# One-hot products in fp32 and columns turned through DRAM in the graph stage of a graph-and-experts kernel

## The chip, the cores and the metric

The kernel runs on one core of one Trainium2 chip. The metric is the time of the whole program on the device, in microseconds (us). TensorE is called PE in the profile, VectorE DVE, ScalarE ACT, GpSimd POOL and SyncE SP. The profile is that of one execution; the time before is the median of three runs.

## The reference

The program has two halves. The first adds to x the product of a sparse matrix (67,584 weighted edges between 2048 nodes, sorted by `dst`) with the normalized rows of x, and a bias per node. The second normalizes the result and adds a mixture of eight experts, of which each row uses its two best.

```python
x = x + gnn(layernorm(x), edge_weight, stack([src, dst]), node_vec1)
x = x + experts(layernorm(x), Wr, br, ln_g, ln_b, W1, b1, W2, b2)

def gnn(x, values, indices, bias):          # x [2048, 256]
    row, col = indices[0], indices[1]       # row is src, col is dst
    gathered = values[:, None] * x[col]
    return segment_sum(gathered, row, num_segments=2048) + bias
```

All is fp32. The change is in the first half alone.

## The kernel before

**The idea of the graph stage.** The sparse matrix is built as a dense one, block by block, and multiplied. For each destination node (a column of the matrix) at most KW = 64 edges are looked at. A source number is split into a high part (32 values, HI) and a low part (64 values, LO). For one destination, `hr` is a 64 x 32 table (edge by high part, holding the edge's weight where the high part agrees) and `hl` a 64 x 64 table (edge by low part, holding one). Their product over the edges is the column's 2048 entries as a 32 x 64 table. To be exact in bf16, the weight is cut into three bf16 parts, and three products are added up for each destination: 2048 x 3 = 6144 products. Each uses a quarter of TensorE's columns and half of its rows (`tile_position`), so that eight tiles stand side by side.

**Finding the edges.** The destinations are handled in GQ = 8 groups of 256 (q). For each group a run of 656 entries of `dst` is gathered for each partition (`get_run`), at a place that `find_run` finds from a coarse list of every 528th entry (`first_i`). ScalarE counts with three Sign passes how many entries lie before the destination (`count_before`), `get_win` works out where its edges begin and gathers 64 sources and 64 weights for each of two destinations by indirect DMAs on GpSimd. `keys_of` makes the high part, the low part and the mask, and `turn_keys` transposes them on TensorE, so that edges lie on partitions. `next_part` makes the second and third bf16 part of the weight.

**The loop.** A half-block n (0 to 31) has 64 destinations. `make_hots(n)` makes `hl`, `eq` and `hr` on VectorE (L335, L338, L342). `make_cols(n)` runs 192 products into `pa` (L360) and copies them to `ar` on ScalarE (L364). After two half-blocks, `turn_cols` transposes `ar` within blocks of 32 x 32 on VectorE (L372) to `ac`, a block of 128 destinations by 2048 sources. `dense(g, b)` multiplies the blocks of a group (GROUPS: one or two blocks) by the normalized rows `xn_sb` for the 128 nodes of block b (L379). In the loop at least 8 such products are put after each half-block. `add_later` copies four results to `sum` on ScalarE (L391), and GpSimd adds them to `acc` by an accumulating DMA (L393). The last group is added on VectorE (L385), after the loop, in steps that alternate with the router of the second half. During n = 0 to 3 the rows of x are also transposed, weighed for the router (`weigh_x`) and normalized (`scale_x`).

**Order.** All this stands in a section whose order on every engine is written by hand (`manual_schedule`): each engine runs its instructions in the order of the program text. The constants ahead of it are placed by the framework. The check at n = NH - 3 uses `rows_d`, a copy of `dst` with one entry more per row: it counts where `dst` falls; if the edges were unsorted or a destination had more than 64, a slow path would be taken.

**After the graph stage.** The router, the lists of rows for each expert, and the expert slots follow (L690 on); the first product there is `px` (L839), then `ph` (L1012) and `py` (L1026).

Of the kernel before, what the change touches and what calls it, by code (L numbers as in the profile page):

```python
# [21 lines left out]
P = 128  # L22
# [4 lines left out]
def kernel(  # L27
# [46 lines left out]
    RUN = EJ + P  # L74
    GROUPS = (1, 1, 2, 2, 2, 2, 2, 2, 2)
# [19 lines left out]
    first_i = xpool.tile([P, 1], I32, name="first_i")  # L95
    nc.sync.dma_start(first_i, dst.rearrange("(p j) -> p j", p=P)[:, 0:1])
# [5 lines left out]
    nc.scalar.dma_start(wr_sb, Wr.rearrange("(k p) e -> p k e", p=P))  # L102
    nv_rows = small.tile([NB, P], F32, name="nv_rows", bufs=1)
    nc.scalar.dma_start(nv_rows, node_vec1.rearrange("(b p) o -> b (p o)", p=P))
    for q in range(4):
        s = slice(q * NB // 4, (q + 1) * NB // 4)
        (nc.sync, nc.scalar)[q % 2].dma_start(acc[:, s, :D], xv[:, s, :])
    b1_rows = small.tile([NE * KH, P], F32, name="b1_rows", bufs=1)
    nc.sync.dma_start(b1_rows, b1.rearrange("e (c p) -> (e c) p", p=P))
    g_rows = small.tile([NE * KD, P], F32, name="g_rows", bufs=1)  # L110
    nc.sync.dma_start(g_rows, ln_g.rearrange("e (k p) -> (e k) p", p=P))
    be_rows = small.tile([NE * KD, P], F32, name="be_rows", bufs=1)
    nc.sync.dma_start(be_rows, ln_b.rearrange("e (k p) -> (e k) p", p=P))
    br_sb = consts.tile([P, NE], F32, name="br_sb")
    nc.scalar.dma_start(br_sb, bass.AP(tensor=br.tensor, offset=br.offset, ap=[[0, P], [1, NE]]))
    rows_d = xpool.tile([P, EJ + 1], I32, name="rows_d")
    nc.vector.memset(rows_d[:, EJ:], N)
    flat = lambda n: bass.AP(tensor=dst.tensor, offset=dst.offset, ap=[[EJ, P - 1], [1, n]])
    nc.sync.dma_start(rows_d[:P - 1, :], flat(EJ + 1))
    nc.sync.dma_start(rows_d[P - 1:, :EJ], dst.rearrange("(p j) -> p j", p=P)[P - 1:, :])  # L120


    ident = consts.tile([P, P], F32, name="ident")
# [9 lines left out]
    iota_p = consts.tile([P, P], F32, name="iota_p")  # L133
    nc.gpsimd.iota(iota_p, pattern=[[1, P]], base=0, channel_multiplier=0,
                   allow_small_or_imprecise_dtypes=True)
    eps_sb = consts.tile([P, 1], F32, name="eps_sb")
    nc.vector.memset(eps_sb, EPS)
# [19 lines left out]
    cols_d = dram.tile([NE, P, KH + 2 * KD], F32, name="cols_d")  # L157
    none = consts.tile([P, RW], F32, name="none")
# [13 lines left out]
    firsts = consts.tile([P, P], F32, name="firsts")  # L172
    nc.gpsimd.iota(firsts, pattern=[[P, 2], [GH // 2, 2], [GH, 4], [GC, GM]], base=0,
                   channel_multiplier=0, allow_small_or_imprecise_dtypes=True)
    col_q = consts.tile([P, GQ], F32, name="col_q")
    nc.gpsimd.iota(col_q, pattern=[[GC * P, GQ]], base=0, channel_multiplier=0,
                   allow_small_or_imprecise_dtypes=True)
    own_p = consts.tile([P, P], F32, name="own_p")
    col_p = consts.tile([P, 1], F32, name="col_p")
    nc.vector.scalar_tensor_tensor(own_p, firsts, 1.0, ident, op0=OP.mult, op1=OP.mult,  # L180
                                   accum_out=col_p)
    col0 = consts.tile([P, GQ], F32, name="col0")
    nc.vector.tensor_scalar(col0, col_q, col_p, None, op0=OP.add)
    edge = consts.tile([P, GQ, 3], F32, name="edge")
    nc.vector.tensor_tensor(edge, col0[:, :, None].to_broadcast([P, GQ, 3]),
                            iota_p[:, None, :3].to_broadcast([P, GQ, 3]), OP.add)
    nc.vector.tensor_scalar(edge, edge, -0.5, None, op0=OP.add)

    cols_1 = gnn.enter_context(tc.tile_pool(name="cols_1", bufs=GROUPS[-1]))
    ps_s = gnn.enter_context(tc.tile_pool(name="ps_s", bufs=3, space=PSUM))
    edges = gnn.enter_context(ExitStack())
    cols_0 = edges.enter_context(tc.tile_pool(name="cols_0", bufs=6))
    pool = lambda name, bufs, **k: edges.enter_context(tc.tile_pool(name=name, bufs=bufs, **k))
    find = pool("find", 1)
    one_d = lambda t: t.rearrange("(e o) -> e o", o=1)
    wins = [None] * GQ
    runs = [None] * GQ
    used_q = find.tile([P, GQ, GC], F32, name="used_q")  # L200
    less = find.tile([P, GQ], F32, name="less")
    base = find.tile([P, GQ], F32, name="base")
    base_i = find.tile([P, GQ], I32, name="base_i")
    mid = find.tile([P, GQ], F32, name="mid")
# [8 lines left out]
    def find_run(pf, q):  # L213
        junk = find.tile([P, P], F32, name="less_1")
        nc.vector.tensor_scalar(junk, pf, col0[:, q:q + 1], None, op0=OP.is_lt, op1=OP.add,
                                accum_out=less[:, q:q + 1])

    def get_runs(q0, q1, q2):
        r = slice(q0, q1)
        nc.vector.tensor_scalar(base[:, r], less[:, r], -1.0, 0.0, op0=OP.add, op1=OP.max)  # L220
        nc.vector.tensor_scalar(base[:, r], base[:, r], float(EJ), float(E - RUN), op0=OP.mult,
# [3 lines left out]
        for q in range(q0, q2):  # L225
            get_run(q)
# [10 lines left out]
    def count_before(q, ends=range(3)):  # L237
        for i in ends:
            sign = find.tile([P, RUN], BF16, name="sign")
            nc.scalar.activation(sign, runs[q], AF.Sign, bias=edge[:, q, i:i + 1], scale=-1.0,  # L240
                                 accum_out=signs[:, q, i:i + 1])

    def get_win(q):
        nc.vector.scalar_tensor_tensor(at[:, q, :], signs[:, q, :], 0.5,
# [103 lines left out]
    def make_cols(n, hl, hr):  # L348
# [3 lines left out]
        if h == 0:  # L352
            ars[cb] = rowsp.tile([P, HI, LO], F32, name="ar")
# [837 lines left out]
```

## Time and profile before

| | us |
|---|---|
| median of three runs | 598.04 (594.74 to 598.71) |
| the profiled execution, its own time | 603.62 |
| its span, first to last instruction | 601.8 |
| first one-hot product (L360) | 34.0 |
| last dense products of the graph stage end | 312.9 |

| engine | busy us | share |
|---|---|---|
| PE | 492.3 | 82% |
| PE weight loads | 416.7 | 69% |
| DVE | 306.1 | 51% |
| ACT | 241.8 | 40% |
| POOL | 176.3 | 29% |

How to read it: busy times are summed over the span, and matmuls are pipelined, so a busy PE is not a PE at its peak. A group of the profile names its line, engine and operation, what is written and read, and then busy time, mean time of one in ns, and the idle time just before its instructions with what ended that ("<-issue" is time in which the engine waited for nothing that the profile shows). PEclk is the granted share of TensorE's clock.

### The profile page before, as it was taken

Reading aid. Unit: us, or ns where it says so; the run is one execution under the profiler, and the core shown is the slowest. Engines: PE = TensorE matmul, PEld = TensorE weight load, DVE = VectorE, ACT = ScalarE, POOL = GpSimd, SP = SyncE. Lnnn points to the kernel's source line nnn. Section 1 sums busy time; section 2 is a strip of 40 time slices with the busy share of each in tenths; the row PEclk is TensorE's granted clock in tenths of the full one; section 3 lists DMA queues with packets and bytes.
Section 4 is the critical chain, followed back from the end, with each engine's and each line's share of the span. In section 5 each row is a group of like instructions: output and inputs, shape, how many; then the busy total and the mean of one; then the engine's idle time right before and its main releaser. Section 6 shows DMA issues by size and latency. Waiting matters only on the chain. (4 is left out here: it accounts for less than half of the span.)

```text
span 601.8 us, 18439 instructions
## 1 busy us (share of the span) xinstructions
PE 492.3 (82%) x8070; PEld 416.7 (69%) x8070; DVE 306.1 (51%) x678; ACT 241.8 (40%) x547; POOL 176.3 (29%) x165
## 2 busy tenths in 40 slices
PE   1168787487887697689989999999999989994792
PEld 1157665476676575567868788888888878883682
DVE  5675977878786776674586642222232232220101
ACT  2436575346364443233593733333333333331220
POOL 2253034234242311111103343333344423431121
PEclk9998588599899897989979999999999999997797
DMA  6011277244444432532995269766689967748332
GB/s 196 20 56 35 43 144 148 40 103 82 100 78 82 84 76 52 98 66 59 248 386 173 43 206 339 227 184 188 200 255 361 312 146 209 186 129 240 104 88 98
DMA packets 55486, 88.53 MB, mean 147 GB/s; under 512 B 8274, under 2 KB 43330, under 8 KB 55330
## 3 DMA queue, kind: packets, MB, share of 16 engines
q1 hardware_dynamic: 40946, 55.20, 27.8%
q0 software_dynamic: 12944, 30.95, 25.6%
q8 instruction: 67, 1.10, 0.8%
q10 hardware_dynamic: 1504, 1.07, 0.6%
q14 instruction: 25, 0.20, 0.1%
HBM read 60.65 MB, written 11.36 MB: 120 GB/s over the span
## 5 line engine op out<-in xcount | busy, mean ns | idle before, releaser
L379 PE MATMUL py<-xn_sb,ac 128*128 128x264 f32 x512 | 144.4, 440 | 8.6 <-ACT sum L391 6.2
L379 PEld LDWEIGHTS py<-xn_sb,ac 128*128 128x128 f32 x512 | 107.7, 217 | 34.3 <-ACT sum L391 10.2
L1012 PE MATMUL ph<-xeT,w 128*128 128x256 f32 (+1 forms) x576 | 123.0, 372 | 3.8 <-issue 2.5
L1026 PE MATMUL py<-w,hT 128*128 128x256 f32 x544 | 124.4, 387 | 0.0
L1014 ACT ACTIVATE hT<-ph,ec 128x256 f32<-128x256 f32 (+1 forms) x144 | 66.6, 462 | 133.8 <-PE ph L1012 75.9
L1012 PEld LDWEIGHTS ph<-xeT,w 128*128 128x128 f32 x576 | 106.0, 194 | 18.0 <-issue 5.0
L1026 PEld LDWEIGHTS py<-w,hT 128*128 128x128 f32 x544 | 104.7, 195 | 14.3
L360 PE MATMUL pa<-hl,hr 64*32 64x64 bf16 x6144 | 62.6, 203 | 46.8 <-issue 39.7
L360 PEld LDWEIGHTS <-hr 64*32 64x32 bf16 x6144 | 54.2, 91 | 59.9 <-issue 51.3
L1034 POOL DMA_INDIRECT y_d<-ys,to_i x32 | 51.8, 1620 | 139.3 <-DVE ys L1029 89.5
L393 POOL DMA_DIRECT2D acc<-sum x32 | 28.8, 912 | 156.8 <-ACT sum L391 156.8
L391 ACT COPY sum<-py 128x264 f32<-128x264 f32 x128 | 47.6, 381 | 56.9 <-PE py L379 55.6
L986 DVE TENSOR_SCALAR xeT<-px,ec 128x256 f32<-128x256 f32 (+1 forms) x40 | 19.1, 519 | 94.9 <-PE px L977 92.2
L372 DVE STREAM_TRANSPOSE ac<-ar 128x2048 f32<-128x2048 f32 x16 | 59.5, 3718 | 2.5 <-ACT ar L364 2.5
L1029 DVE SCALAR_TENSOR_TENSOR ys<-py,wt,b2w 128x256 f32<-128x256 f32 x34 | 16.4, 484 | 80.0 <-PE py L1026 73.4
L342 DVE TENSOR_TENSOR hr<-eq,w 128x3072 bf16<-128x3072 bf16 x32 | 56.3, 1758 | 1.1
L944 POOL DMA_INDIRECT xs<-xr_d,to_i x39 | 40.8, 1045 | 52.9 <-DVE z L723 31.2
L364 ACT COPY ar<-pa 128x1024 f32<-128x1024 f32 x32 | 32.3, 1009 | 54.5 <-PE pa L360 54.5
L335 DVE TENSOR_TENSOR hl<-k,iota_b 128x2048 bf16<-128x2048 bf16 x32 | 38.8, 1213 | 27.8 <-PE pa L360 27.5
L1001 ACT ACTIVATE b2w<-b,wt 128x256 f32<-128x256 f32 x37 | 16.8, 500 | 44.4 <-DVE wt L999 39.9
L252 POOL DMA_INDIRECT win_s<-in_src,at_i x16 | 18.6, 1162 | 45.3 <-DVE n_d L262 42.3
L240 ACT ACTIVATE sign<-run,edge 128x656 bf16<-128x656 int32 x24 | 20.4, 848 | 7.7 <-DMA run<-in_dst,base_i 7.2
(205 smaller groups left out, 348.4 us busy)
## 6 DMA issues: line engine op xcount, KB each, us to landing
w<-in_L_ffn_W SPq DMA_DIRECT2D x42, 1024.0 KB, 7.3
acc<-sum POOLq DMA_DIRECT2D x32, 528.0 KB, 5.5
b<-in_L_ffn_b SPq DMA_DIRECT2D x21, 128.0 KB, 8.1
out<-y_d SPq DMA_DIRECT2D x4, 512.0 KB, 5.3
xr_d<-rec SPq DMA_DIRECT2D x1, 1300.0 KB, 7.6
y_d<-acc SPq DMA_DIRECT2D x1, 1280.0 KB
acc<-in_x SPq DMA_DIRECT2D x2, 512.0 KB, 6.1
acc<-in_x ACTq DMA_DIRECT2D x2, 512.0 KB, 7.9
```

Source lines behind the costliest of these rows:

```text
L335: nc.vector.tensor_tensor(hl.rearrange("p g (n t) -> p g n t", t=2), two(k2[:, 0], g, LO), pair(iota_b, LO), OP.is_equal)
L342: nc.vector.tensor_tensor(hr.rearrange("p g i (n t) -> p (g i) n t", t=2), eq[:, :, None, :].to_broadcast([P, GH, 3, HI]), w[:, :, None, : ...
L360: nc.tensor.matmul(pa[c * HI:(c + 1) * HI, j, m * LO:(m + 1) * LO], hr[k, c * GM + m, i, :], hl[k, c * GM + m, :], start=(i == 0), stop=(i ...
L364: nc.scalar.copy(ars[cb][:, h * HI // 2:(h + 1) * HI // 2, :].rearrange("p (m j) l -> p j m l", j=GC), pa.rearrange("p j (m l) -> p j m l" ...
L372: nc.vector.transpose(acs[cb].rearrange("p h l -> p l h"), ars[cb].rearrange("p d l -> p l d"))
L379: nc.tensor.matmul(pa[:, :DX], acs[c].rearrange("p h l -> p (h l)")[:, b * P:(b + 1) * P], xn_sb[:, c, :], start=(c == group_of[g][0]), st ...
L391: nc.scalar.copy(sums_of[0][:, k, :], pa[:, :DX])
L944: nc.gpsimd.indirect_dma_start(out=(sets[s.set][0] if into is None else into)[:, t, :], out_offset=None, in_=(xr_d if rows is None else ro ...
L1012: nc.tensor.matmul(ph, w1[:, k, c * P:(c + 1) * P], xeT[:, k, :], start=(k == 0), stop=(k == KD - 1))
L1014: nc.scalar.activation(hT[:, c, :s.n * P], ph, AF.Gelu, bias=ec[:, c:c + 1], scale=1.0)
L1026: nc.tensor.matmul(py, hT[:, c, t * P:(t + 1) * P], w2[:, c, :], start=(c == 0), stop=(c == KH - 1))
L1034: st = nc.gpsimd.indirect_dma_start(out=y_d[:, :], out_offset=bass.IndirectOffsetOnAxis(ap=tos[s.to][:, t:t + 1], axis=0), in_=ys, in_offs ...
```

## The change

- One product in fp32 for each destination replaces the three in bf16. `hl` is made in bf16 (`hb`) and widened to fp32 by ScalarE; `hr` is fp32. `next_part` and the bf16 parts go.
- A half-block is made in two halves (`make_cols(n, 0)` and `make_cols(n, 1)`), with dense products after each of them (QUOTA = 8 in all). The dense results are added by VectorE (`add`), not by ScalarE and an accumulating DMA. GROUPS has larger last groups, and a group becomes ready LAG = 4 half-blocks after its last block began.
- The columns are turned through DRAM (`move_cols`): SP stores `ar` to `ad`, and reads it back in four parts of 16 rows, in pieces of 64 elements.
- Destinations are in plain order (`col0`, `base` from iota). Runs of q = 0 are read at fixed places (`run_0`, STEP apart) by SP, and `count_before`, `locate` and `get_half` work on one edge at a time; the other runs are shorter (264 + 128 entries) and found from a list of every 264th entry.
- Loads of the start are in another order on SP and ACT; the memset of the last column of `rows_d` stands after its load. Statistics and scaling of x are done four blocks at a time inside the loop, and `node_vec1` is added by GpSimd.

```diff
-    RUN = EJ + P
-    GROUPS = (1, 1, 2, 2, 2, 2, 2, 2, 2)
+    EH = EJ // 2
+    RUN = EH + P
+    STEP = E // NG
+    BACK = 4 * STEP
+    RUN_0 = 2 * BACK + P
+    LAG = 4
+    QUOTA = 8
+    GROUPS = (1, 1, 2, 2, 3, 3, 4)
...
+    nc.sync.dma_start(run_0[nf:, :], part(dst, 0, STEP, P - nf, RUN_0))
+    nc.sync.dma_start(run_0[:nf, :], part(dst, 0, 0, nf, RUN_0))
+    nc.sync.dma_start(first_i, bass.AP(tensor=dst.tensor, offset=dst.offset, ap=[[EJ, P], [EH, 2]]))
...
+    get_x(nc.sync, 0)
+    get_x(nc.scalar, 1)
+    nc.sync.dma_start(wr_sb, Wr.rearrange("(k p) e -> p k e", p=P))
     nc.sync.dma_start(b1_rows, b1.rearrange("e (c p) -> (e c) p", p=P))
     nc.sync.dma_start(g_rows, ln_g.rearrange("e (k p) -> (e k) p", p=P))
     nc.sync.dma_start(be_rows, ln_b.rearrange("e (k p) -> (e k) p", p=P))
+    nc.sync.dma_start(nv_rows, node_vec1.rearrange("(b p) o -> b (p o)", p=P))
+    get_x(nc.sync, 2)
+    get_x(nc.sync, 3)
+    nc.sync.dma_start(br_sb, bass.AP(tensor=br.tensor, offset=br.offset, ap=[[0, P], [1, NE]]))
-    nc.vector.memset(rows_d[:, EJ:], N)
-    nc.sync.dma_start(rows_d[:P - 1, :], flat(EJ + 1))
+    nc.sync.dma_start(rows_d[:P - 1, :], part(dst, 0, EJ, P - 1, EJ + 1))
     nc.sync.dma_start(rows_d[P - 1:, :EJ], dst.rearrange("(p j) -> p j", p=P)[P - 1:, :])
...
+    nc.vector.memset(rows_d[:, EJ:], N)
...
     def make_hots(n):
-        hl = hotl.tile([P, GH, LO], BF16, name="hl")
-        nc.vector.tensor_tensor(hl.rearrange("p g (n t) -> p g n t", t=2),
+        hb = hotl.tile([P, GH, LO], BF16, name="hb")
+        nc.vector.tensor_tensor(hb.rearrange("p g (n t) -> p g n t", t=2),
                                 two(k2[:, 0], g, LO), pair(iota_b, LO), OP.is_equal)
+        hl = hotl.tile([P, GH, LO], F32, name="hl")
+        casts.append(lambda: nc.scalar.copy(hl, hb))
         eq = hotr.tile([P, GH, HI], BF16, name="eq")
...
-        hr = hotr.tile([P, GH, 3, HI], BF16, name="hr")
...
+        hr = hotr.tile([P, GH, HI], F32, name="hr")
+        nc.vector.tensor_tensor(hr, eq, w_t[:, g * GH:(g + 1) * GH, None]
+                                .to_broadcast([P, GH, HI]), OP.mult)
...
-    def make_cols(n, hl, hr):
+    def make_cols(n, i, hl, hr):
+        if i == 0:
+            halves_of[n] = (ps_a.tile([P, GC, GM * LO], F32, name="pa"),
+                            rowsp.tile([P, GM, GC, LO], F32, name="ar"))
+        pa, ar = halves_of[n]
+        ms = range(i * GM // 2, (i + 1) * GM // 2)
+        for m in ms:
+            for c in range(4):
+                for j in range(GC):
+                    k = slice(j * KW, (j + 1) * KW)
+                    nc.tensor.matmul(pa[c * HI:(c + 1) * HI, j, m * LO:(m + 1) * LO],
+                                     hr[k, c * GM + m, :], hl[k, c * GM + m, :],
+                                     start=True, stop=True, tile_position=(j * KW, c * HI))
+        ms = slice(ms.start, ms.stop)
+        nc.scalar.copy(ar[:, ms].rearrange("p m j l -> p j m l"),
+                       pa.rearrange("p j (m l) -> p j m l", l=LO)[:, :, ms])
+
+    def move_cols(n):
+        cb, h = n // 2, n % 2
+        ar = halves_of.pop(n)[1]
+        ad = dram.tile([P, GM * GC, LO], F32, name="ad", bufs=4)
+        nc.sync.dma_start(ad, ar.rearrange("p m j l -> p (m j) l"))
+        if h == 0:
+            acs[cb] = (cols_1 if cb >= NB - GROUPS[-1] else cols_0).tile([P, HI, LO], F32, name="ac")
+        for c in range(4):
+            d = h * P // 2 + c * GM * GC
+            nc.sync.dma_start(acs[cb][d:d + GM * GC],
+                              ad[c * HI:(c + 1) * HI].rearrange("h k l -> k h l"))
...
-    def turn_cols(cb):
-        nc.vector.transpose(acs[cb].rearrange("p h l -> p l h"),
-                            ars[cb].rearrange("p d l -> p l d"))
...
-    def add_later(b, pa):
...
+    for q in range(2, GQ):
+        find_run(pf, q)
+    place_runs()
+    get_run(1)
+    get_run(2)
+    cols, wc = turn_columns()
+    block_stats(bn, mv, acc, range(0, 2))
+    turn_x(0)
+    turn_x(2)
+    turn_keys(0, keys_of(0))
...
+        for n in range(NH + 1):
+            while late:
+                add(*late.pop(0))
+            if n < NH:
+                make_cols(n, 0, *hots[n])
+            if n + 1 < NH:
+                hots[n + 1] = make_hots(n + 1)
+                casts.pop()()
+            while ready < last_g and 2 * group_of[ready][-1] + LAG <= n:
+                jobs += [(ready, b) for b in range(NB)]
+                ready += 1
+            more_dense(n)
+            if n < NH:
+                make_cols(n, 1, *hots.pop(n))
+                move_cols(n)
+            while late:
+                add(*late.pop(0))
+            for s in range(1, GQ):
+                if n == max(4 * s - 6, 0):
+                    count_before(s)
+                if n == max(4 * s - 5, 0):
+                    get_win(s)
+                    if s + 2 < GQ:
+                        get_run(s + 2)
+                if n == 4 * s - 2:
+                    turn_keys(s, keys_of(s))
+            if n < 4:
+                if n:
+                    turn_x(4 * n)
+                    turn_x(4 * n + 2)
+                    block_stats(bn, mv, acc, range(4 * n, 4 * n + 4))
+                scale_x(4 * n, 4)
+                weigh_x(4 * n)
+                weighed_x(4 * n, 4)
+            more_dense(n)
```

In the changed file `run_0` is loaded at L115 and L116, `rows_d` at L145 and L146, its memset is L194, the key transposes are L331 and L332, the one-hot products L370, the ar copy L374, the store L383, the reads L388 and the dense products L395.

## Prediction

> **What bounds the kernel now.** I read the stages first, the busy time of each engine in four stretches:
>
> ```profile
> core 0: us, PE busy (x) PEld busy (x) DVE busy (x) ACT busy (x) POOL busy (x), PEclk, DMA share, GB/s
> 34.00:76.40 42.40, 34.90 (x889) 30.48 (x893) 29.97 (x54) 23.53 (x53) 10.43 (x10) 0.76 0.22 52
> 76.40:285.00 208.60, 164.97 (x5795) 133.03 (x5794) 155.08 (x164) 94.29 (x215) 54.74 (x52) 0.89 0.43 86
> 285.00:313.00 28.00, 24.90 (x109) 20.13 (x110) 18.49 (x44) 19.54 (x50) 2.65 (x5) 0.91 1.02 304
> 313.00:602.00 289.00, 261.92 (x1270) 229.00 (x1269) 81.36 (x316) 93.15 (x204) 96.72 (x75) 0.95 0.66 196
> ```
>
> The change touches the first 313 us: a start of 34 us, half-blocks n = 0 to 3 in 42.4 us, n = 4 to 31 in 208.6 us (7.45 us each), and a tail of 28 us to the first px product. Nothing after that is edited. In the long stretch TensorE and VectorE are both three quarters busy and neither is full, so I read the groups (busy, mean ns of one, idle before it and who ended that) and then TensorE's timeline (start, length, instruction, idle before it):
>
> ```profile
> L379 PE MATMUL py<-xn_sb,ac 128*128 128x264 f32 x512 | 144.4, 440 | 8.6 <-ACT sum L391 6.2
> L360 PE MATMUL pa<-hl,hr 64*32 64x64 bf16 x6144 | 62.6, 203 | 46.8 <-issue 39.7
> L391 ACT COPY sum<-py 128x264 f32<-128x264 f32 x128 | 47.6, 381 | 56.9 <-PE py L379 55.6
> L372 DVE STREAM_TRANSPOSE ac<-ar 128x2048 f32<-128x2048 f32 x16 | 59.5, 3718 | 2.5 <-ACT ar L364 2.5
> L342 DVE TENSOR_TENSOR hr<-eq,w 128x3072 bf16<-128x3072 bf16 x32 | 56.3, 1758 | 1.1
> L364 ACT COPY ar<-pa 128x1024 f32<-128x1024 f32 x32 | 32.3, 1009 | 54.5 <-PE pa L360 54.5
> L335 DVE TENSOR_TENSOR hl<-k,iota_b 128x2048 bf16<-128x2048 bf16 x32 | 38.8, 1213 | 27.8 <-PE pa L360 27.5
> ```
>
> ```profile
> 108.09 1.28 PE L360 MATMUL pa<-hl,hr 64*32 64x64 bf16 x128 [3.94 <-issue]
> 111.82 1.30 PE L360 MATMUL pa<-hl,hr 64*32 64x64 bf16 x128 [2.45 <-issue]
> ...
> 173.59 1.75 PE L360 MATMUL pa<-hl,hr 64*32 64x64 bf16 x192
> ```
>
> Undisturbed, 192 one-hot products take 1.75 us, 8.1 ns from start to start. But 39.7 us are lost to "issue", in bursts of exactly 128 products that begin 3.73 us apart. VectorE in turn waits 27.5 us for these products before hl. So the stretch is bound by the two in turn: VectorE's hl, eq, hr and transposes cost 5.5 us per n, and TensorE's products, when their instructions come late, hold up the next hots.
>
> **What the skill says.** (1) "Runtime: NRT & Kernel Launch", section Instruction fetch mechanics: TensorE's instructions arrive in blocks of 256. The bursts agree: 128 products and 128 weight loads are 256 instructions, and one block takes 3.73 us here. The page calls this mostly hidden; 39.7 us say otherwise. (2) "FP8 and Floating Point Precision", section TensorE Precision Notes: true fp32 is four passes. The trace agrees: an fp32 product is two matmul records (L379 has 512 for 256 products), and 32 records of 256 columns follow each other in 6.91 us, 216 ns each or 0.844 ns a column. (3) "TensorE: Matmul & The Clock Gate", Part 3: products in different tiles overlap, but start in program order. The 8.1 ns agrees, far under the 27 ns that 64 bf16 columns need. (4) "DMA: Bandwidth & Descriptors", section on why a DMA increments its semaphore by 16: a transfer over 127 partitions runs on one DMA engine. The trace agrees (last part of the start, below).
>
> **Products (removed 6144 bf16, added 2048 fp32).** Each fp32 product is two records on the same tile, one after the other. The second can't start until the first has streamed 64 columns at 0.844 ns = 54 ns; the next product is on another tile and may follow a few ns later. So about 54 + 5 = 59 ns per product, whatever the tiles overlap, 64 x 59 = 3.78 us per n. Bounds: 16 ns if the four instructions are limited by issue alone (half of 8.1 ns each); about 86 ns if the second weight load (27 ns) doesn't hide. I take 59: in the full-array stream the next weight load starts beside the running product. Fetch falls from 384 to 256 instructions per n, with the dense products 288, or 4.2 us at 3.73 us per 256: the issue stall goes.
>
> **Steady n (28 of them).** TensorE: 3.78 us of one-hot, 8 dense products of 2 x 221 ns = 3.54 us, and now two changes of tile mode each way instead of one. In the trace the first record after dense to one-hot comes 316 ns on instead of 221, one-hot to dense 127 ns; a round trip is 0.22, two are 0.44. Sum 7.76. By GROUPS, LAG and QUOTA, n = 8, 9, 18, 19 have no dense work; there 6 us. A new stall: at n = 6, 10, ... 26 the key transposes stand between the second half and its dense products, and their f waits for ACT: copy of ar 0.59, two away 0.6, h_1 0.3, then f 0.48 on VectorE, with hand-overs 2.2; the transposes and their mode change 0.8 more; 6 x 3.0 = 18 us. Sum 24 x 7.76 + 4 x 6 + 18 = 228, against 208.6: +19.6.
>
> **Other engines beside it.** VectorE per n: hb 1.21, eq 0.68, hr in fp32 about 1.2 (1024 elements at twice the bf16 slope; bounds 0.7 and 1.8), adds at 0.43 each, 3.4 us at worst (groups of one) and 1.7 with two; keys 0.55: 5.3 to 7.1, under 7.76. The adds are a new wait: they wait for the dense products, and behind them on VectorE stand the hots of n + 1; but these dense products end just before the first half of n, so the hots have all of n. So the 59.5 us of transposes and the smaller hr are freed where they no longer decide. ACT: cast 2048 elements at the slope of its copies (585 ns for 512, 1009 for 1024) 1.86, two ar copies 1.17, keys and signs 1.0: 4.0. The sums on ACT and their accumulating DMAs on POOL (28.8 us) go; POOL's 16 adds of node_vec1 have no row of their kind; between 0.4 us (VectorE's 0.36) and 1.1 (its own iota of that size) each they are hidden, since acc is not added to before n = 4. SP: per n one store of ar (0.4 to issue; stores of 256 to 780 KB landed in 3.9 to 4.1), a wait, four reads of 0.5 each: 0.45 + 4.0 + 2.0 + 0.2 = 6.7 us in a chain, under 7.76 but not by much. The next store stands behind these reads on SP, and ar has two buffers: ACT's ar copy of n + 2 waits for the store of n, and behind that copy stand the cast of hl and the second half's products. So this chain becomes the bound if TensorE is faster than I think. Bandwidth: 2048 pieces of 256 B at 17 ns (window gathers: 138 ns per packet of eight) over 16 engines 2.2 us, and 128 pieces of 4 KB at 159 ns 1.3: half of the time.
>
> **Start.** Reading run 0 at fixed places makes its windows land near 16 us instead of 22. But the memset of rows_d moved behind the load of rows_d, and in VectorE's order it stands among find_run's scans, ahead of place_runs, keys and hots. That load covers 127 partitions:
>
> ```profile
> GB/s 0 2 84 285 328 353 370 362 358 349 128 259 25 23 25 25 23 54 52 30 54 54 6 0 0 0 0 0 0 0 0 33 0 33 0 47 2 33 0 252
> ```
>
> ```profile
> 5.19 0.28 SPq L119 DMA_DIRECT2D rows_d<-in_dst  x1
> 8.71 4.40 SPq L120 DMA_DIRECT2D rows_d<-in_dst  x1
> ```
>
> Slices of 1 us: from 12 us on 25 GB/s is left, one engine's rate; its 127 packets run from 8.8 to 22.0 us. Before, nobody waited. After, it is issued thirteenth on SP, each load from the eighth on waiting for an earlier one: about 8.5, so it lands near 25. Then four scans 2.3, place_runs 0.8, statistics 1.2, keys to k2 3.1 and hots 3.1: first product at 35.5 (was 34.0). n = 0 to 3 are then carried by ACT: 4 x (xn 2.4, xT 1.2, ar 1.2, cast 1.9, small copies 0.5) = 29, signs and keys 6, hand-overs from statistics to sd to rs 1.5 each: 41. So n = 4 starts at 76.5, as before (76.4): no gain.
>
> **Tail.** The last group has 4 columns (64 products) instead of 2 (32). From the last one-hot product: ar copy and store and reads 8.7 us, beside which the rest of n = 31 and three products run; 37 more products for the first ten blocks 16.4; from there to px 10.9, as in the trace (301.7 to 312.7). 36 against 27.7: +8.2.
>
> **Sum.** Start and n = 0 to 3 +0.1, steady +19.6, tail +8.2: +28 on the profiled execution, 603.6 to 632. That execution is 5.6 over the median of the runs shown, so 598 + 28 = 626.
>
> **Rivals.** B, faster: the two records of a product interleave with other tiles', TensorE needs 5 us per n, and SP's chain of 6.7 is the bound: 28 x 6.7 = 188 instead of 228, 586 (557 with stores landing a microsecond sooner). For it: 8.1 ns shows wide overlap, fetch eases. Against: two records of one tile. It decides from about 43 ns per product down, where the 28 us are used up. C, slower still: a product takes 86 ns, 64 x 27 ns x 28 = 48 more, 674; or the reads of 256 B stretch SP's chain to 10 us: 280 + tail, about 678. The dense stream speaks against the first, the gathers' 17 ns against the second. D: rows_d lands before VectorE comes to it; the start gains 11: 615. Against: 13 us on one engine.
>
> **Chances.** Forecast 0.50 (own range 608 to 645), B 0.22, C 0.15, D 0.13. The range leaves out half of B and most of C: 582 to 660. A measurement tells about 1% from no change: faster 0.20 (most of B), within 1% 0.10 (the rest of B, edges), slower 0.70.
>
> **What would show it.** VectorE idle before L194 until about 25 us, the first L370 near 35; L370 starting 59 ns apart on average, no issue gaps; n about 7.8 us; idle of TensorE before L331. I am wrong if 64 products take under 2.8 us, if SP's wait between L383 and L388 exceeds 5 us, or if L194 doesn't wait.

## The result, and the profile after

The changed kernel takes 625.74 us (median of 4 runs, 623.86 to 626.97) beside 596.79 us for the kernel before (4 runs): a ratio of 1.048, 95% interval 1.043 to 1.053. The forecast was 626. The number was right, the main reason for it was not: two errors of the sum cancelled. Ratios and their intervals leave out executions more than 1.5% above the fastest of the same kernel; the medians hold them all.

The profiled execution took 626.97 us with a span of 625.2. The stages come first, cut at the first one-hot product, at n = 4 and at the last one-hot product:

```profile
core 0: us, PE busy (x) PEld busy (x) DVE busy (x) ACT busy (x) POOL busy (x), PEclk, DMA share, GB/s
36.50:75.40 38.90, 30.09 (x603) 26.90 (x603) 22.20 (x65) 28.67 (x57) 22.67 (x21) 1.00 0.55 107
75.40:289.00 213.60, 163.65 (x3957) 121.99 (x3961) 126.88 (x245) 99.98 (x152) 34.63 (x29) 0.86 0.88 141
289.00:325.00 36.00, 19.31 (x115) 15.34 (x105) 5.12 (x14) 4.79 (x15) 0.53 (x3) 0.81 0.98 243
325.00:625.20 300.20, 273.91 (x1344) 239.39 (x1342) 91.14 (x346) 104.28 (x229) 96.50 (x75) 0.96 0.64 191
```

The reader is to see three things. The start up to n = 4 is as long as before (75.4 against 76.4 us). The stretch of n = 4 to 31 takes 213.6 us, only 5 more than before, though TensorE, VectorE and ACT are all less than fully busy; what has doubled is the share of the DMA engines, 0.43 before and 0.88 now (the sum of the packets' times over the time of 16 engines; it can pass 1). And the first px product comes at 339.2 us, 50 us after the last one-hot product, against 28 before. The tail lost 22 us.

The whole profiled executions differ by 23.4 us (601.8 and 625.2), the medians by 29.0: the profiled execution of the kernel before took 603.62 us, 6.8 over its median. So the losses by stage may each be read some microseconds too small.

The waits of the long stretch (engine, line, what it waited for: us in total, times, longest) name the new bound:

```profile
ACT ar L374 <- DMA ad<-ar: 76.1, 17, 6.7
DVE acc L401 <- PE py L395: 64.9, 39, 5.8
PEld pa L370 <- ACT ar L374: 41.7, 21, 4.6
PE pa L370 <- ACT ar L374: 34.6, 16, 4.3
DVE f L321 <- ACT h L317: 11.7, 5, 4.0
```

ACT's copy of ar waits for a store of ar, and TensorE's one-hot products wait for that copy. Why the store is late is on SP's queue (start, length, line, DMAs in a row):

```profile
161.94 2.18 SPq L388 DMA_DIRECT2D ac<-ad  x4
164.22 0.43 SPq L383 DMA_DIRECT2D ad<-ar  x1
169.56 1.89 SPq L388 DMA_DIRECT2D ac<-ad  x4
171.55 0.44 SPq L383 DMA_DIRECT2D ad<-ar  x1
177.46 1.89 SPq L388 DMA_DIRECT2D ac<-ad  x4
179.44 0.43 SPq L383 DMA_DIRECT2D ad<-ar  x1
```

SP never rests for want of work: each store begins 0.1 us after the four reads ahead of it, for every n from 9 on. Between the store and its reads it stands still for 4.5 to 7.2 us, median 5.2, until the store has landed. One round is 0.43 + 5.2 + 1.9 and the small gaps; the stores are 7.96 us apart on average (median 7.90). TensorE's timeline of the same stretch shows what it could do:

```profile
160.26 0.86 PE L370 MATMUL pa<-hl,hr 64*32 64x64 f32 x64
161.05 2.05 PE L395 MATMUL py<-xn_sb,ac 128*128 128x264 f32 x8
163.03 0.86 PE L370 MATMUL pa<-hl,hr 64*32 64x64 f32 x64
...
170.22 0.86 PE L370 MATMUL pa<-hl,hr 64*32 64x64 f32 x64 [1.34 <-ACT ar L374]
...
178.18 0.86 PE L370 MATMUL pa<-hl,hr 64*32 64x64 f32 x64 [2.35 <-ACT ar L374]
```

Where nothing waits, a half of a half-block (32 one-hot products, which are 64 records, and four dense ones) goes from 160.26 to 163.03, 2.77 us, so 5.54 us per n. The 64 records start within 0.643 us, on average 10 ns apart and 20 ns a product. The groups that the sum used (busy, mean ns of one, idle before it) are

```profile
L349 ACT CAST hl<-hb 128x2048 f32<-128x2048 bf16 x32 | 60.8, 1901 | 3.9 <-DVE hb L346 3.8
L370 PE MATMUL pa<-hl,hr 64*32 64x64 f32 x4096 | 63.9, 253 | 43.5 <-ACT ar L374 38.8 <-DVE hr L354 3.7 <-issue 0.7
L354 DVE TENSOR_TENSOR hr<-eq,w_t 128x1024 f32<-128x1024 bf16 x32 | 39.2, 1225 | 4.6 <-PE pa L370 2.6
L374 ACT COPY ar<-pa 128x512 f32<-128x512 f32 x64 | 37.4, 585 | 107.1 <-DMA ad<-ar 76.1 <-PE pa L370 22.3 <-PE py L395 8.6
```

The bursts that end in "issue" are gone, as forecast: 0.7 us of idle time before L370 ends so, against 39.7 before. What stands before L370 now is ACT's copy, and what stands before that is the store.

The start shows the wait that the prediction named (VectorE, then SP). The profile names no releaser for the 12.37 us; that the memset L194 is behind it is shown by moving it (e3 below):

```profile
27.23 0.48 DVE L225 TENSOR_SCALAR_CACHE_REDUCE less<-py,col 128x256 f32<-128x256 f32 x1 [12.37 <-issue]
27.25 0.06 DVE L194 MEMSET rows_d<- 128x1 int32 x1
```

```profile
11.76 0.29 SPq L145 DMA_DIRECT2D rows_d<-in_dst  x1
12.10 6.53 SPq L146 DMA_DIRECT2D rows_d<-in_dst  x1
```

The tail is on TensorE's timeline:

```profile
289.39 1.60 PE L395 MATMUL py<-xn_sb,ac 128*128 128x264 f32 x6
292.94 1.78 PE L395 MATMUL py<-xn_sb,ac 128*128 128x264 f32 x6 [1.94 <-DMA ac<-ad]
309.46 25.69 PE L395 MATMUL py<-xn_sb,ac 128*128 128x264 f32 x106 [14.75 <-DMA ec<-cols_d]
335.58 3.81 PE L395 MATMUL py<-xn_sb,ac 128*128 128x264 f32 x16
339.22 2.11 PE L852 MATMUL px<-chosen,rec 128*128 128x256 f32 x9
```

TensorE stands for 14.75 us ahead of the last group's products. The releaser named is a load of ec, but what those products need is the last column: its store was issued at 297.1 us, its reads up to 304.1. The last one-hot product had ended at 289.5 and its copy to ar at 290.1, so the store came 7.0 us after its data were ready: SP was nearly one whole round behind.

### The profile page after: what moved, and what is told of

The parts are those of the page before. It is cut to its first block, busy times and chain, and to the rows that moved or that the text cites. A ratio compares the mean times of both kernels' runs of the same rounds, so it can differ in the third digit from the quotient of the medians.

```text
span 625.2 us, 14595 instructions
## 1 busy us (share of the span) xinstructions
PE 492.8 (79%) x6022; PEld 407.6 (65%) x6022; DVE 258.7 (41%) x731; ACT 246.9 (39%) x470; POOL 162.2 (26%) x148
## 3 DMA queue, kind: packets, MB, share of 16 engines
q0 software_dynamic: 8144, 12.37, 9.9%
## 4 chain that ended last, share of the span: by engine, by line
PE 44%; DMA 31%; DVE 7%; ACT 7%; SPq 5%; issue 5%; POOL 0%; POOLq 0%; ACTq 0%; DVEq 0%
DMA ad<-ar 21%; PE py L1039 16%; PE ph L1025 15%; PE py L395 6%; SPq L388 5%; DMA xs<-xr_d,to_i 4%; ACT hl L349 3%; DMA y_d<-ys,to_i 3%; PE pa L370 1%; PE px L852 1%; DVE acc L401 1%; ACT ar L374 1%; DMA run<-in_dst 1%; PE px L990 1%; DMA out<-y_d 1%
## 5 line engine op out<-in xcount | busy, mean ns | idle before, releaser
L395 PE MATMUL py<-xn_sb,ac 128*128 128x264 f32 x512 | 143.4, 432 | 19.0 <-DMA ec<-cols_d 14.7
L395 PEld LDWEIGHTS py<-xn_sb,ac 128*128 128x128 f32 x512 | 102.5, 210 | 43.4 <-issue 17.4
L1039 PEld LDWEIGHTS py<-w,hT 128*128 128x128 f32 x544 | 105.3, 196 | 14.3
L370 PE MATMUL pa<-hl,hr 64*32 64x64 f32 x4096 | 63.9, 253 | 43.5 <-ACT ar L374 38.8
L370 PEld LDWEIGHTS pa<-hl,hr 64*32 64x32 f32 x4096 | 51.1, 120 | 65.9 <-ACT ar L374 46.8
L401 DVE TENSOR_TENSOR acc<-acc,py 128x264 f32<-128x264 f32 x112 | 45.2, 425 | 96.5 <-PE py L395 96.4
L374 ACT COPY ar<-pa 128x512 f32<-128x512 f32 x64 | 37.4, 585 | 107.1 <-DMA ad<-ar 76.1
L349 ACT CAST hl<-hb 128x2048 f32<-128x2048 bf16 x32 | 60.8, 1901 | 3.9 <-DVE hb L346 3.8
L354 DVE TENSOR_TENSOR hr<-eq,w_t 128x1024 f32<-128x1024 bf16 x32 | 39.2, 1225 | 4.6 <-PE pa L370 2.6
L346 DVE TENSOR_TENSOR hb<-k,iota_b 128x2048 bf16<-128x2048 bf16 x32 | 39.0, 1218 | 1.3 <-ACT k L335 1.2
L1014 ACT ACTIVATE b2w<-b,wt 128x256 f32<-128x256 f32 x37 | 16.8, 500 | 48.5 <-DVE wt L1012 43.4
L331 PE MATMUL pk<-ident,f 128*128 128x128 f32 x16 | 6.7, 416 | 29.9 <-ACT h L317 15.7
L331 PEld LDWEIGHTS pk<-ident,f 128*128 128x128 f32 x16 | 2.6, 163 | 33.4 <-ACT h L317 16.1
```

The source lines that it names most:

```text
L346: nc.vector.tensor_tensor(hb.rearrange("p g (n t) -> p g n t", t=2), two(k2[:, 0], g, LO), pair(iota_b, LO), OP.is_equal)
L349: casts.append(lambda: nc.scalar.copy(hl, hb))
L354: nc.vector.tensor_tensor(hr, eq, w_t[:, g * GH:(g + 1) * GH, None] .to_broadcast([P, GH, HI]), OP.mult)
L370: nc.tensor.matmul(pa[c * HI:(c + 1) * HI, j, m * LO:(m + 1) * LO], hr[k, c * GM + m, :], hl[k, c * GM + m, :], start=True, stop=True, til ...
L374: nc.scalar.copy(ar[:, ms].rearrange("p m j l -> p j m l"), pa.rearrange("p j (m l) -> p j m l", l=LO)[:, :, ms])
L395: nc.tensor.matmul(pa[:, :DX], acs[c].rearrange("p h l -> p (h l)")[:, b * P:(b + 1) * P], xn_sb[:, c, :], start=(c == group_of[g][0]), st ...
```

## Experiments

The twelve runs fall in four sets, each beside runs of the kernel before. In the table all times are read from the profiled executions: the first ar copy of n = 4, the last one-hot product, the first px product, and the differences (loop and tail). The kernel before copies ar once for each n, so its loop is compared in the stages above only.

| kernel | n = 4 | last one-hot | px | loop | tail | median us | ratio to before |
|---|---|---|---|---|---|---|---|
| before | | 284.8 | 312.7 | | 27.9 | 596.79 | 1 |
| changed | 76.8 | 289.2 | 339.2 | 212.4 | 50.0 | 625.74 | 1.048 |
| set 1: e1_store_ahead | 82.4 | 288.7 | 332.1 | 206.3 | 43.4 | 616.50 | 1.009 |
| set 1: e2_double | 96.5 | 385.1 | 427.4 | 288.6 | 42.3 | 716.59 | 1.173 |
| set 1: e3_memset_first | 71.5 | 285.7 | 336.1 | 214.2 | 50.4 | 625.03 | 1.021 |
| set 1: e4_plain_reads | 83.0 | 279.6 | 328.2 | 196.6 | 48.6 | 637.66 | 1.040 |
| set 2: e0_after | 76.3 | 289.0 | 339.8 | 212.7 | 50.8 | 626.81 | 1.045 |
| set 2: e5_last_one | 76.8 | 289.6 | 333.9 | 212.8 | 44.3 | 622.13 | 1.039 |
| set 2: e6_vector_turn | 87.2 | 315.4 | 351.9 | 228.2 | 36.5 | 638.32 | 1.065 |
| set 2: e7_three | 65.1 | 250.8 | 291.5 | 185.7 | 40.7 | 580.31 | 0.964 |
| set 3: e8_ahead_again | 76.6 | 260.3 | 305.1 | 183.7 | 44.8 | 594.87 | 0.999 |
| set 3: e9_ahead_memset | 65.8 | 252.3 | 296.1 | 186.5 | 43.8 | 584.94 | 0.979 |
| set 3: e10_quarter | 66.6 | 266.6 | 306.0 | 200.0 | 39.4 | 591.79 | 0.996 |
| set 4: e11_ahead_plain | 76.6 | 256.3 | 298.4 | 179.7 | 42.1 | 604.84 | 1.017 |

The first set lay in a slower stretch of the machine: the kernel before took 615.65 us there (604.45 to 626.27) and 600.09, 596.97 and 596.28 in sets 2 to 4. So its kernels are compared with each other only, and what mattered was run again. Sets 1 and 2 ran on one chip, sets 3 and 4 on two others; between sets 2 to 4 the kernel before moved by 0.6%, and comparisons across them are no finer than that.

### The changed kernel again: e0

> The changed kernel itself, unaltered, beside the others of this set: 622 to 630. In the one-hot products of the kernels run so far beside another set of runs of the kernel before, 11 to 13 us of idle time of TensorE ended in no release that the profile shows (instruction supply), against 0.7 us in the first profile of the changed kernel. If that comes from those edits, this run shows 0.7 again; if it comes from the runs, it shows 10 or more.

626.81 us, 1.045 (1.039 to 1.052), and 1.3 us of idle time of TensorE before one-hot products that ended in "issue". The 11 to 13 us of the first set were not there, so that set's own runs have a share in them.

### The store issued ahead: e1 and e8

```diff
-        cb, h = n // 2, n % 2
...
         ad = dram.tile([P, GM * GC, LO], F32, name="ad", bufs=4)
         nc.sync.dma_start(ad, ar.rearrange("p m j l -> p (m j) l"))
+        stored.append((n, ad))
+        if len(stored) > 1:
+            read_cols()
+
+    def read_cols():
+        n, ad = stored.pop(0)
+        cb, h = n // 2, n % 2
...
                 move_cols(n)
+                if n == NH - 1:
+                    read_cols()
```

> SP issues the store of ar for half-block n first and then the four reads of n-1, whose store has had a whole half-block to land; nothing else changes. Theory S (SP's chain of issue, store's landing of 5.8 us and four reads sets the period of 7.6 us): the wait between L383 and the reads goes, the period falls to the next bound; if that is the DMA engines (share 0.88 of 7.6 us = 6.7 us) 28 x 0.9 = 25 us less and up to 10 us less in the tail, 590 to 602; if it is TensorE (5.3 us of work) or VectorE, 570 to 585. Theory T (TensorE's own work sets the period, as the prediction had it): 626 within 3 us, since TensorE has the same instructions.

The first run gave 616.50 us, a ratio of 1.009 (1.006 to 1.013). SP's wait was gone, yet the mean distance of the stores fell only to 7.47 us: TensorE's one-hot products came in trickles of three to six records every 0.7 us, 11.2 us of idle time before them ended in "issue", and ACT's copies waited for the products instead. That left open whether the edit or the set was the cause, so it was run again.

> Only the store of n issued ahead of the reads of n-1, a second time. Its first run lay beside runs of the kernel before at 615.65 us, with more idle time of TensorE that ended in no release, and its period of 7.7 us hardly fell; together with two other edits the period was 6.86 us. If the gain in the period is this edit's own (the DMA engines then full at 1.04 of their time), 588 to 596 with n = 4 to 31 at 6.9 us each; if it needs the other edits, 612 to 620 again.

The second run gave 594.87 us, 0.999 (0.995 to 1.004): the whole loss of the change is gone, with one reordering on SP. The loop took 183.7 us instead of 212.7 in e0_after, 6.6 us per n, and the tail 44.8 instead of 50.8. SP's queue shows how:

```profile
157.43 2.80 SPq L394 DMA_DIRECT2D ac<-ad  x4
163.30 0.34 SPq L382 DMA_DIRECT2D ad<-ar  x1
163.73 2.62 SPq L394 DMA_DIRECT2D ac<-ad  x4
168.91 0.34 SPq L382 DMA_DIRECT2D ad<-ar  x1
```

The reads follow the store of the next n at once, and SP then waits for TensorE's and ACT's work, not they for SP. The theory that TensorE sets the period, which is the prediction's, forecast 626 for this kernel and falls. What slowed the first run beyond the store's order isn't known; the kernel before was slower by 3.1% in that set, and e1 by 3.6% against e8.

### Products doubled: e2

```diff
-                    nc.tensor.matmul(pa[c * HI:(c + 1) * HI, j, m * LO:(m + 1) * LO],
+                    for _ in range(2):
+                        nc.tensor.matmul(pa[c * HI:(c + 1) * HI, j, m * LO:(m + 1) * LO],
...
```

> Each one-hot product is run twice in a row, into the same place with the same result. Theory S (SP's chain is the bound; 64 products take 1.3 us and TensorE has about 2 us to spare in each half-block of 7.6 us): 624 to 634. Theory T (TensorE is the bound): 32 x 1.3 = 42 us more, 668; and if a product costs the predicted 59 ns, 32 x 3.78 = 121 more, 747.

It gave 716.59 us, 1.173 (1.160 to 1.186), and fits neither theory. Where nothing waits, TensorE's timeline (same columns) has

```profile
99.16 1.86 PE L371 MATMUL pa<-hl,hr 64*32 64x64 f32 x128
100.96 2.05 PE L396 MATMUL py<-xn_sb,ac 128*128 128x264 f32 x8
102.93 1.86 PE L371 MATMUL pa<-hl,hr 64*32 64x64 f32 x128
...
113.64 0.96 PE L371 MATMUL pa<-hl,hr 64*32 64x64 f32 x54 [1.95 <-issue]
```

From 99.16 to 102.93 is 3.77 us instead of 2.77: the 32 extra products cost 1.00 us, 31 ns each although every one follows another on the same tile, and not 59. That would be 7.5 us per n, just inside SP's round. But the stores came 10.5 us apart on average, and part of that goes to something that neither theory had counted, the supply of instructions. Their DMA queue has, in this kernel's page and in that of e0_after,

```profile
q8 instruction: 82, 1.34, 0.9%
```

```profile
q8 instruction: 51, 0.84, 0.6%
```

packets, MB and share. 31 packets more of 16 KB, about one for 256 of the 8192 added instructions (records of products and of weight loads). In the loop there were 58 of them, one every 5 us, and 37.2 us of TensorE's idle time before one-hot products ended in "issue" there (47.5 in the whole run). Such waits held the kernel before, and doubling brings them back. By the sum they are about half of the 77 us that the loop took beyond 7.5 us per n; the rest isn't resolved. So the experiment gives the price of a product, but is no clean test of TensorE's slack.

### The memset of rows_d: e3 and e9

```diff
+    nc.vector.memset(rows_d[:, EJ:], N)
     nc.sync.dma_start(rows_d[:P - 1, :], part(dst, 0, EJ, P - 1, EJ + 1))
     nc.sync.dma_start(rows_d[P - 1:, :EJ], dst.rearrange("(p j) -> p j", p=P)[P - 1:, :])
...
-    nc.vector.memset(rows_d[:, EJ:], N)
```

> The memset of the last column of rows_d stands ahead of the load of rows_d, so that the load waits for it and not VectorE for the load. Start theory: VectorE no longer waits the 12 us to 27 us, the first one-hot product comes at 25 to 28 us instead of 36.6, and all of it is carried to the end: 613 to 618. Rival: what follows in VectorE's order (runs of q = 1, 2, the columns, the keys) waits for loads and gathers that land at 25 us anyway: 622 to 627.

The first one-hot product came at 25.1 us instead of 36.6, as forecast, and n = 4 at 71.5, where e1 and e4 of that set, with the start unchanged, had 82.4 and 83.0. The ratio was 1.021 (1.013 to 1.028); with the set's unrest, this alone doesn't tell how much of it reaches the end.

> Store ahead and the memset of rows_d ahead of its load; GROUPS as in the changed kernel. Start theory: 10 to 12 us less than the run with the store ahead alone, since the first product comes at 25 instead of 36.5 us and nothing later takes it back: 577 to 586. And the difference to the run with all three edits (580.31) is what the last group of one brings: 3 to 8 us by its own run. Rival: with the DMA engines full, an earlier start is taken back in the loop, less than 5 us.

With the store ahead as well: 584.94 us, 0.979 (0.959 to 0.998), 9.9 us under the run with the store ahead alone, in the same set. First product 25.6 against 36.6, n = 4 at 65.8 against 76.6, px at 296.1 against 305.1. The loop gives back 2.8 of the 10.8; the rest reaches px.

### Pieces of the reads: e4 and e11

```diff
-                              ad[c * HI:(c + 1) * HI].rearrange("h k l -> k h l"))
+                              ad[c * HI:(c + 1) * HI].rearrange("(k a) b l -> k (a b) l", a=2))
```

> The four reads of ad take the same bytes from the same quarter of ad into the same rows of ac, in plain order: pieces of 8 KB instead of 256 B, the columns are not turned. The order of issue and the waits on SP stay. Bandwidth theory (the 256-byte pieces of the reads load the DMA engines, and the next store's landing waits behind them): the landing falls from 5.8 toward 4.1 us, the period from 7.6 to about 5.9, 570 to 590, and the DMA share falls under 0.5. Latency theory (the landing of a store of 512 KB is what it is, the pieces don't matter): 620 to 626.

SP's median wait for the store was 4.6 us, against 5.2 in e3_memset_first, which has SP's round unchanged in the same set; the stores were 7.36 us apart instead of 8.05, and the loop took 196.6 instead of 214.2. So the size of the pieces lengthens the next store's landing by 0.6 us, a third of what the bandwidth theory wanted. The total of 637.66 us is not to be compared: with the columns not turned, the rows go to other experts, and 640 instead of 576 of the later ph records were run.

> The store issued ahead, and the reads in plain order, 8 KB a piece instead of 256 B: the same bytes from the same quarter of ad, the columns not turned, so that the nodes are routed otherwise after the loop and only the loop's own times are compared (183.7 us from the first ar copy of n = 4 to the last one-hot product with the store ahead alone, DMA engines at 1.01). DMA theory: 64 pieces at 740 ns and 128 of 4 KB at 200 ns over 16 engines are 4.6 us a half-block instead of 6.3, the share falls under 0.85 and the loop to 150 to 170 us, TensorE's 5.3 us a half-block and its instructions being next. Rival: TensorE's instruction supply or VectorE, not the DMA engines, holds the period of 6.8 us: 178 to 186 us.

Whether full DMA engines are the next bound once the store is ahead is read from the stages of e8_ahead_again and e11_ahead_plain, in this order:

```profile
76.80:260.50 183.70, 155.45 (x3915) 115.38 (x3914) 126.90 (x245) 99.83 (x148) 34.04 (x28) 0.90 1.02 168
```

```profile
76.60:256.30 179.70, 157.13 (x3918) 117.51 (x3918) 126.62 (x245) 100.23 (x148) 33.44 (x28) 0.91 0.75 172
```

The share falls from 1.02 to 0.75, the loop by 4 us. The DMA theory wanted 150 to 170 and falls, the rival's 178 to 186 holds; full engines alone didn't hold the period. (The total of 604.84 us has the longer second half of e4, 640 ph records, and is not to be compared.) TensorE is busy for 155 us of 184 in e8_ahead_again, its own 5.54 us per n by the timeline make 155, and the rest is spread over small waits (ar copies, keys, instruction supply), of which none was taken away by itself.

### The last group: e5

```diff
-    GROUPS = (1, 1, 2, 2, 3, 3, 4)
+    GROUPS = (1, 1, 2, 2, 3, 3, 3, 1)
```

> GROUPS (1, 1, 2, 2, 3, 3, 3, 1) instead of (1, 1, 2, 2, 3, 3, 4): columns 12 to 14 become ready with the last one-hot product, and only 16 dense products are left for after the last reads. Tail theory (from the last one-hot product to the router 49.7 us, of which 20 are SP's lag, store and reads with TensorE idle for 14.7, and 30 the rest of 64 products and the counts): the 48 products of columns 12 to 14 run in those 20 us, the rest shrinks from 30 to 10 or 15 us: 606 to 612. Rival: the dense products of the last columns wait for SP's reads of column 14, two periods late, and run no earlier: 620 to 627.

622.13 us, 4.7 under e0_after. TensorE's idle time ahead of the dense products fell from 13.8 us to 2.5, yet px came only 5.8 us sooner:

```profile
294.74 22.40 PE L395 MATMUL py<-xn_sb,ac 128*128 128x264 f32 x92 [2.54 <-DMA ac<-ad]
318.95 6.50 PE L395 MATMUL py<-xn_sb,ac 128*128 128x264 f32 x28 [1.81 <-DVEq L601]
330.70 0.22 PE L773 MATMUL counts<-sel,before 128*128 128x80 bf16 x1 [5.25 <-DVE seen_b L761]
```

Then TensorE waited for VectorE: the router's counts, whose preparation had run beside the dense products, now held it up for 5.25 us. The forecast of 15 to 20 us took the freed time for gain without asking what came next.

### The turn on VectorE: e6

```diff
+    perm = consts.tile([P, P], F32, name="perm")
...
-            nc.tensor.transpose(pk[:, i, :], f[:, i, :], ident)
+            nc.tensor.matmul(pk[:, i, :], f[:, i, :], perm, start=True, stop=True)
...
-        nc.sync.dma_start(ad, ar.rearrange("p m j l -> p (m j) l"))
...
+        if h:
+            acs[cb] = (cols_1 if cb >= NB - GROUPS[-1] else cols_0).tile([P, HI, LO], F32, name="ac")
+            nc.vector.transpose(acs[cb].rearrange("p h l -> p l h"),
+                                ars.pop(cb).rearrange("p m j l -> p l (m j)"))
```

> The columns are turned by VectorE again (one transpose of 3.72 us for each column of two half-blocks, as in the kernel before) instead of by way of DRAM; the key columns are brought into the order that this needs by a product with a permutation in place of the transposes by the identity; all else is the changed kernel's. Chain theory (SP's store, wait and reads set the period of 7.8 us and the late tail): the chain goes, VectorE's 3.1 of hots, 1.9 of transposes, 1.5 of adds and 0.5 of keys are then about 7.0 us a half-block: 28 x 0.8 = 22 us less in the loop, 12 to 15 less in the tail: 588 to 595. Rival (TensorE's instruction supply sets 7.5 us anyway, as it did with the store issued ahead): only the tail gains, 608 to 614. If the DRAM turn costs nothing: 626.

638.32 us, 11.5 over e0_after: the way through DRAM is cheaper here than the transposes, for all its round. The tail did gain 14.3 us, but the loop took 228.2, and n = 4 came at 87.2. Its groups and its waits (the second fence, from 80 to 300 us) say why:

```profile
L391 DVE STREAM_TRANSPOSE ac<-ar 128x2048 f32<-128x2048 f32 x16 | 67.8, 4235 | 20.5 <-ACT ar L381 20.5
```

```profile
ACT hl L353 <- DVE hb L350: 41.1, 12, 5.0
PEld pk L335 <- DVE f L323: 21.7, 6, 5.6
PEld py L398 <- DVE acc L404: 17.4, 6, 4.9
```

The edit also leaves xT three buffers instead of four; ACT's and TensorE's waits about xT are as in e0_after. The late n = 4 goes with the statistics of x, for which ACT waits 11.0 us before it, against 1.7 in e0_after. A transpose takes 4.24 us here (3.72 before) and VectorE stands for 20.5 us more, because a transpose waits for the copy of ar with all other work queued behind it. Hots, keys and adds come late, and TensorE waits for each in turn. The expected 7.0 us per n was a sum of busy times and had left those waits out.

### All three, and one column in four on VectorE: e7 and e10

> Three edits together: store of n ahead of the reads of n-1, memset of rows_d ahead of its load, GROUPS with a last group of one. If their gains are in different places they add: about 3 to 5 us at the start, 15 to 20 us in the tail, 0 to 5 in the loop, 597 to 607. If the loop also gains because the chain on SP is gone: under 597.

580.31 us, 0.964 (0.955 to 0.973): faster than both kernels, 46.5 us under e0_after in the same set. In its profile n = 4 comes 11.2 us sooner than in e0_after, the loop is 27.0 us shorter, the tail 10.1; the gains lie in different places and add.

> The three edits together, and one column in four (3, 7, 11, 15) turned by VectorE, with no store and no reads; the key columns are ordered by a product with a permutation for that. DMA theory (with the store ahead, 2048 pieces of 256 B at 37 ns and 128 of 4 KB at 200 ns over 16 engines, 6.3 us, and the rest set the period of 6.86 us): a quarter of it goes, the mean period falls to 5.6 to 6.2, 555 to 572. Rival: VectorE's 4.2 us per turned column, in front of the adds and the next hots, stall TensorE by as much as is won: 575 to 590.

On top of that, a quarter of the columns turned by VectorE (the edit of e6, for cb % 4 == 3 only): 591.79 us, 0.996 (0.992 to 1.000), so 11 us lost and not won against e7, and 7 against e9_ahead_memset in the same set, which has the larger last group. In its profile, of an execution of 594.35 us, the DMA share fell to 0.82, but the loop grew from 185.7 to 200.0 us; VectorE stood for 7.6 us before its four transposes of 4.27 us, and ACT for 12.5 us for hb behind them. The rival expectation had the mechanism, and with 575 to 590 still put the loss too low.

## Why the prediction came out

**Products: the step that failed.** "The second can't start until the first has streamed 64 columns ... the next product is on another tile and may follow a few ns later. So about 54 + 5 = 59 ns per product, whatever the tiles overlap". Measured: 20 ns, 1.3 us per n and not 3.78. Records start 10 ns apart on average, so the next product does not wait for 54 ns of streaming. With 108 ns for the two records of a product (the prediction's own 2 x 54) and a new product each 20 ns, about five are under way at a time, by estimate. Whether the two records of one product overlap on their tile isn't seen in the trace. Even two products in a row on one tile (e2) cost 31 ns more, not 59. No run shows the 27 ns for a weight load in the upper bound of 86. The prediction had named "64 products under 2.8 us" as what would refute it, and that is what came.

**Steady n: wrong bound.** TensorE was put at 7.76 us per n and is at 5.54. The loop was to lose 19.6 us and lost 5. The stall of the key transposes, put at 18 us, was 12.1 in the loop, and SP's round went on beside it.

**SP's chain: the term that was mis-sized.** "0.45 + 4.0 + 2.0 + 0.2 = 6.7 us in a chain, under 7.76": the issues were right (0.43 and 1.9), the landing was not. SP waited 5.2 us after the issue; from the issue on, as the 4.0 was read, the store took 5.9. The round was 8.0 us on average (median 7.9). The 4.0 came from three stores of 256 to 780 KB and passed over one of that range in the same view of the kernel before (size, us to landing):

```profile
y_d<-acc SPq DMA_DIRECT2D x1, 768.0 KB, 9.0
```

The wait is long where the reads of the half-block before were issued 0.1 us ahead of the store. In e2_double the stores lie farther apart: the ten that were issued more than 5 us after the last reads held SP for 2.3 to 4.0 us, median 2.4, against 5.3 for the 26 of the changed kernel that stood right behind their reads. One of the ten:

```profile
178.65 0.34 SPq L384 DMA_DIRECT2D ad<-ar  x1
181.29 1.89 SPq L389 DMA_DIRECT2D ac<-ad  x4
```

With 8 KB pieces (e4) the wait was still 4.6, so the size of the pieces accounts for 0.6 of it, and the larger part points to the reads' traffic itself. That part is a comparison of stores, no run was made for it. A period priced with the landing of other stores leaves out the load that the chain puts on itself.

The estimate of 17 ns for a piece of 256 bytes was low: in the loop it takes 37 ns on average. The Trainium skill, "DMA: Bandwidth & Descriptors", section Why small descriptors are slow (HBM only), states a fixed overhead per packet, 27% of the time of one of 256 bytes. The trace shows more: a piece of 8 KB took 736 ns in e4, 23 ns for each 256 bytes of it, so 14 of the 37 ns, 38%, go with the small size. Nor is 37 ns a fixed price: in e2_double, with a DMA share of 0.58 in its loop, the median piece took 18 ns, against 35 in the changed kernel.

**Rival B was the mechanism.** It said that TensorE needs 5 us and SP's chain binds, and priced it at 586. Correct it by the loop (213.6 - 188 = 26 us) and by the tail (50.0 - 36 = 14 us) and it gives 626. Two of the prediction's three signs of being wrong came, the fast products and SP waiting over 5 us between L383 and L388. The forecast of 626 had overestimated the loop by 14 to 15 us and underestimated the tail by as much: that the number came out was luck. Rival C's reads that stretch SP's round to 10 us got it to 8.0; its product of 86 ns and rival D's early landing of rows_d did not come.

**Start: right.** The memset waited until 27.25 us (25 forecast) behind a load that was issued at 11.76, not 8.5; the first product came at 36.6 (35.5) and n = 4 at 75.4 (76.5). Undone, it is worth 9.9 us (e9 against e8).

**Tail: the second term that was mis-sized.** "ar copy and store and reads 8.7 us": from the last one-hot product to the first product of the last group that could run on, it was 20 us (289.5 to 309.5). The sum took SP to be free; being the bound, it was nearly a round behind, and its store came 7.0 us late. The other 4 us are the longer landing of the store and of the reads. The rest of the tail, 29.8 us, was near the forecast 27.3.

**Beside the path: right.** hr took 1.225 us (1.2 forecast), the cast of hl 1.901 (1.86), a copy of ar 0.585. The idle time that ends in "issue" went, as the one-hot instructions per n fell from 384 to 256, one block. The Trainium skill, "Runtime: NRT & Kernel Launch", section Instruction fetch mechanics, gives the block's size as 256, and e2's packets agree with it (31 for 8192 instructions). It comes back where TensorE is no longer held up by SP (5.5 us before one-hot products from 80 to 260 us in e8).

So the change by itself didn't pay, because the wait for the store was put between two issues on one queue. Its products in fp32 and its turn by DRAM did not have to cost time: with the next store in that wait, the same work runs as fast as before, and with two small edits more it is 3.6% faster than the kernel before.

## What to carry to other kernels

A queue that issues a transfer, waits for it to land and issues what depends on it has a period of its own; add up issue, landing and the dependent issues, take the landing from transfers under the load to come, and if it is near the other engines' period, issue the next store before the dependent reads. When a queue is the bound, it is also late at the end: count its lag in the tail, not a free queue. And before pricing a new instruction from the length of one record, ask how many of them stream beside each other.

## What was not expected of the hardware

- fp32 products of 64 rows by 32 columns on eight tiles start 10 ns apart by record, 20 ns by product; in a pair on the same tile the second costs 31 ns.
- A store of 512 KB right behind 512 KB of reads held the queue for 5.3 us, one issued over 5 us after the last reads for 2.4 (medians, changed kernel and e2).
- A 16 KB packet of instructions took 1.3 us on average in the loop of the changed kernel and 1.6 with a DMA share of 1.02 (e8). The profile counts these packets to the same 16 engines as the data. The share alone doesn't set their time: with 0.58 (e2) it was 1.4.
- Full DMA engines (1.02) and a quarter less (0.75) gave nearly the same period (e8 and e11): the share of the engines' time is no proof of a bound.
